# Attention logits of heads 1 to 7 by way of a DRAM row, an earlier load of two vectors, and two sums moved, in a two-layer graph attention kernel

## The chip, the core and the metric

The kernel runs on one core of one Trainium2 chip. The metric is the device time of one launch in microseconds (us). A core has TensorE (PE, with its weight loads shown apart as PEld), VectorE (DVE), ScalarE (ACT), GpSimd (POOL) and SyncE (SP, which here only issues DMAs), and 16 DMA engines that all queues share. Each engine runs its own instructions in order and waits for others on semaphores.

## The reference

A residual block over 512 nodes with 768 features: `layernorm(x + GAT(x))`, where GAT has two attention layers over the same edges. The first has 8 heads, whose outputs stand side by side (512 x 6144), the second one head.

```python
h = (x @ W).reshape(n, H, C)
alpha_s = jnp.einsum('nhc,hc->nh', h, a_s)          # source logits
alpha_d = jnp.einsum('nhc,hc->nh', h, a_d)          # destination logits
e = jax.nn.leaky_relu(alpha_s[src] + alpha_d[dst], NEG_SLOPE)
m = jax.ops.segment_max(e, dst, num_segments=n)
e = jnp.exp(e - m[dst])
denom = jax.ops.segment_sum(e, dst, num_segments=n)
alpha = e / (denom[dst] + EPS)
out = jax.ops.segment_sum(h[src] * alpha[:, :, None], dst, num_segments=n)
...
h = jax.nn.elu(gat_layer(x, W1, a_src1, a_dst1, b1, edge_index, concat=True))
out = gat_layer(h, W2, a_src2, a_dst2, b2, edge_index, concat=True)
```

## The kernel before

The edges are turned once into a dense 512 x 512 matrix of counts, `cnt`, with a mask `absent` beside it. Each head is then dense work: its projection, a 512 x 512 matrix of attention weights, their product, ELU, and its part of the second layer's product, which is summed over the heads in `h2` and `u2`. Nodes lie in 4 tiles of 128 partitions.

The attention matrix of a head needs the destination logit of a node as one value for each partition (`AL[h][1]`) and the source logits of all 512 nodes along the free axis, the same on every partition (`BC[h]`). The source logits come out of VectorE as a 128 x 4 tile, `AL[h][0]`. `spread(h)` (L360) makes `BC[h]` from it on TensorE: four transposes of a column that is broadcast to 128 x 128, into one PSUM bank. Then for each tile of nodes `lift` (L366, ACT: destination minus source logits), `leak` (L372, DVE), `rank` (L375, DVE and an exponential on ACT) and `weigh` (L525, DVE, with `cnt` as factor). `turn_out` and `turn_in` transpose the result by DMA into `PT`.

Large products are done by Strassen's scheme in the form with seven products: `left`, `right`, `left_sums` and `right_sums` return the operands and a list of VectorE sums that some of them need. `second` and `projection` return 14 pairs each, of a product and of the VectorE or ScalarE step that empties its bank. P2 is added to the bank of P1, so P2 waits until the step that empties P1 has read it; P4 and P3 stand likewise on P7 and P5.

The order of the work is written out by hand: the program's order is each engine's order, and there is no scheduler. The loop over `h` (L678), here called pass 0 to pass 6, does this:

1. SP issues the weights `load_w1(h + 2)`: `w2t` (the piece t1) and six rows of blocks, each 384 KB, into buffers that the products of the projection before must have left. POOL issues two more DMAs that add onto what has landed (L104, L115).
2. `mixed` (L603): attention product of head `h` and ELU. Between its steps VectorE takes entries of the list `fill`: the sums that are still open and the logits of head `h + 1` (`half_logits`, L256). After it `load_a` loads the logit vectors of head `h + 2`. The last pass, 6, uses `aggregate` instead of `mixed`; VectorE then does the logits of head 7 and twelve products of the second layer's vectors with rows of its weights (L703), which fill `V`.
3. `second(h)`: its pairs P1 are issued (`m()`), then on VectorE the step that empties the first bank (`pairs[0][1]`), the last ELU steps (`finish`), the sums `gsums[0]` and `gsums[1]`, and the step for the second bank (`pairs[1][1]`, L306, or L304 where the bank starts a sum). TensorE does `spread(h + 1)` after its P1 products, then the two products of P2, P6, P7, P4, P5, P3. The attention matrix of head `h + 1` is made beside them.
4. The projection of head `h + 2`.

In pass 0 the start differs: the last products of head 1's projection (L667 on) run beside the end of head 0's attention matrix, and the lists `beside` set what VectorE and ScalarE do at each of them. `rsums` are four sums over `PT` that the second product of `mixed(0)`, P6, needs the first two of. `some_logits` are two half logits of head 1.

In pass 6 SP issues `load_w2(7)` (t1 and six blocks), then the two vectors `a_src2` and `a_dst2` of the second layer (L686). All SP loads stand in one queue; DMA issues of SP rotate through eight semaphores, so that a DMA is not issued before the one eight places ahead of it has landed.

Of the kernel before, what the change touches and what calls it, by code (L numbers as in the profile page):

```python
# [8 lines left out]
F32 = mybir.dt.float32  # L9
# [3 lines left out]
U16 = mybir.dt.uint16  # L13
# [23 lines left out]
def gat_pass(  # L37
# [16 lines left out]
    nc = tc.nc  # L54
    P = 128
    N, D = x.shape
    H = a_src1.shape[0]
    E = src.shape[0]
    NT = N // P
# [11 lines left out]
    keep = ctx.enter_context(tc.tile_pool(name="keep", bufs=1))  # L71
    wpool = ctx.enter_context(tc.tile_pool(name="weights", bufs=1))
    hpool = ctx.enter_context(tc.tile_pool(name="hpool", bufs=2))
    small = ctx.enter_context(tc.tile_pool(name="small", bufs=4))
    qpool = ctx.enter_context(tc.tile_pool(name="qpool", bufs=4))
    counting = ExitStack()
    ohp = counting.enter_context(tc.tile_pool(name="onehot", bufs=1))
    mm = ctx.enter_context(tc.tile_pool(name="mm", bufs=5, space=bass.MemoryType.PSUM))
    tr = ctx.enter_context(tc.tile_pool(name="tr", bufs=2, space=bass.MemoryType.PSUM))
    bc = ctx.enter_context(tc.tile_pool(name="bc", bufs=1, space=bass.MemoryType.PSUM))  # L80
    def row_bcast(ap_row):
        return bass.AP(tensor=ap_row.tensor, offset=ap_row.offset, ap=[[0, P], [1, D]])

# [12 lines left out]
    def load_w(W, h, slot, m):  # L98


        t1 = wpool.tile([P, HK, HALF], F32, name=f"{slot}t1")
        upper = m[:HK * P, :].rearrange("(k p) d -> p k d", p=P)
        nc.sync.dma_start(t1, upper[:, :, L])
        nc.gpsimd.dma_start(t1, upper[:, :, R], accum_op=ALU.add)  # L104
        W[h] = []
        for r in range(2):
            w = wpool.tile([P, HK, D], F32, name=f"{slot}{r}")
            for k in range(r * HK, (r + 1) * HK):
                nc.sync.dma_start(w[:, k - r * HK, :], m[k * P:(k + 1) * P, :])
            W[h].append(w)  # L110
        W[h].append(t1)

        def rest():

            nc.gpsimd.dma_start(W[h][0][:, :, R], m[HK * P:, R].rearrange("(k p) d -> p k d", p=P),  # L115
                                accum_op=ALU.add)
        return rest
# [4 lines left out]
    def load_w2(h, slot="w1"):  # L122
        return load_w(W2, h, slot, w2[h * D:(h + 1) * D, :])
# [81 lines left out]
        nc.vector.scalar_tensor_tensor(below, rel, float(W), below, op0=ALU.is_ge, op1=ALU.add,  # L205
                                       accum_out=stray)

    cnt = keep.tile([P, NT, N], F32, name="cnt")
    absent = keep.tile([P, NT, N], BF16, name="absent")
    xT = keep.tile([P, DC, N], F32, name="xT")  # L210
    xS = keep.tile([P, 3, HK, HN], F32, name="xS")
# [11 lines left out]
    def left(aT, s):  # L223
        a11, a12 = aT[:, :HK, :HN], aT[:, HK:, :HN]
        a21, a22 = aT[:, :HK, HN:], aT[:, HK:, HN:]
        tt = nc.vector.tensor_tensor
        return dict(P1=a11, P2=a12, P3=s[:, 2], P4=a22, P5=s[:, 0], P6=s[:, 1], P7=a21), [
            lambda: tt(s[:, 0], a21, a22, op=ALU.subtract),
            lambda: tt(s[:, 1], s[:, 0], a11, op=ALU.subtract),
            lambda: tt(a21, a11, a21, op=ALU.subtract),  # L230
            lambda: tt(s[:, 2], a12, s[:, 1], op=ALU.add),
        ]
# [18 lines left out]
    HS, AL, BC = {}, {}, {}  # L251
# [108 lines left out]
    def spread(h):  # L360
        BC[h] = bc.tile([P, 512], F32, name="bc")
        for t in range(NT):
            nc.tensor.transpose(BC[h][:, t * P:(t + 1) * P],  # L363
                                AL[h][0][:, t:t + 1].to_broadcast([P, P]), ident)

    def lift(h, t):  # L366

# [30 lines left out]
    if not general:  # L398
# [5 lines left out]
        cps, done = {}, 0  # L404
# [111 lines left out]
    late = ctx.enter_context(tc.tile_pool(name="late", bufs=1))  # L516
# [35 lines left out]
    def turn_in(t):  # L552
        nc.scalar.copy(PT.rearrange("p s n -> p (s n)").bitcast(U16).rearrange("p (s n h) -> p s n h", s=NT, h=2)[  # L553
            :, :, t * P:(t + 1) * P, :], parted.pop(t).rearrange("p (h s d) -> p s d h", h=2, s=NT))
# [99 lines left out]
    AA, lsums = left_sums(0)  # L654
    BB, rsums = right_sums()
    some_logits = half_logits(1, 2)

    def give(t):
# [3 lines left out]
    done = {n: (lambda n=n: pairs[n][1]()) for n in range(4, 13)}  # L662
    beside = {4: [lambda: give(0)], 5: [done[4]], 6: [done[5]], 7: [done[6], lambda: give(1)],
              8: [done[7], lambda: leak(q[3]), lambda: rank(q[3], 3), lambda: turn_in(0)], 9: [lambda: give(2), done[8]],
              10: [lambda: give(3), lambda: turn_in(1), done[9]], 11: [done[10], lsums[0]],
              12: [done[11], lambda: turn_in(2), *lsums[1:3]], 13: [done[12], some_logits[0], lambda: turn_in(3)]}
    for n in range(4, 14):  # L667
        pairs[n][0]()
        for f in beside[n]:
# [2 lines left out]
            load_w2(0)()  # L672
            B2, pending = right(W2[0], "w1")
    pairs[13][1]()
    for f in rsums:
        f()
    besides = [lsums[3], some_logits[1]]
    for h in range(H - 1):  # L678
        if h + 2 < H:
            load_w1(h + 2)()  # L680
        else:
            last_sum = load_w2(H - 1, "w2")
            A[H] = []
            for j, a in ((2, a_src2[0]), (4, a_dst2[0])):
                v = wpool.tile([P, HK, HALF], F32, name=f"w2t{j}").rearrange("p k n -> p (k n)")[:, :D]
                nc.sync.dma_start(v, row_bcast(a))  # L686
                A[H].append(v)
        GA, gsums = left(gT, gS)
        if h + 2 < H:
            finish = mixed(h, AA, BB, besides + [p for t in ((0, 1) if h else (0, 1, 3)) for p in half_logits(h + 1, t)])  # L690
        else:
            finish = []
            for c in range(DC):
                finish.append(aggregate(h, c))
                if c:
                    finish.pop(0)()
                if c < 2:
                    logits(h + 1, HS[h + 1], c)
                else:

                    for k in ((0, 1), (2,), (3,), (4, 5))[c - 2]:
                        for v, a, sign in zip(range(2), A[H], (1.0, -1.0)):
                            nc.vector.scalar_tensor_tensor(scr, W2[H - 1][k // HK][:, k % HK, :], sign, a,  # L703
                                                           op0=ALU.mult, op1=ALU.mult, accum_out=V[:, k, v:v + 1])
        besides = []
        if h + 2 < H:
            load_a(h + 2, a_src1[h + 2], a_dst1[h + 2])
        pairs = second(h, GA, B2)
        for m, _ in pairs[:2]:
            m()  # L710
        pairs[0][1]()
        for f in finish:
            f()
        gsums[0]()
        gsums[1]()
        pairs[1][1]()
        if pending:
            pending.pop(0)()
        spread(h + 1)
        pairs[2][0]()  # L720
        gsums[2]()
        pairs[3][0]()
        gsums[3]()
        if pending:
            pending.pop(0)()
        pairs[2][1]()
        pairs[3][1]()
        last = h + 2 == H
        q = [lift(h + 1, 0)]
        for n in range(2, 7):  # L730
            (m0, e0), (m1, e1) = pairs[2 * n:2 * n + 2]
            m0()
            if not last:
                m1()
            if n < 6:
                leak(q[n - 2])
                rank(q[n - 2], n - 2)
            if n < 5:
                q.append(lift(h + 1, n - 1))
            if last:  # L740

                if n > 3:
                    turn(q[n - 4], n - 4)
                if n == 6:
                    weigh(q[3], 3)
                m1(lambda: turn(q[3], 3) if n == 6 else None)
            if not last and n == 6:
                turn_in(0)
                weigh(q[2], 2)
                turn_out(q[2], 2)  # L750
            e0()
            if last and 2 < n < 6:
                weigh(q[n - 3], n - 3)
            if not last and 3 < n < 6:
                weigh(q[n - 4], n - 4)
                turn_out(q[n - 4], n - 4)
            if not last and n == 6:
                weigh(q[3], 3)
                turn_out(q[3], 3)
                load_w2(h + 1)()  # L760
            e1()
        if h + 2 < H:
            B_, sums = right(W1[h + 2], "w2")
            pairs = projection(h + 2, XA, B_)
            for n in range(14):
                pairs[n][0]()
                if n == 0:
                    turn_in(1)
                    B2, sums2 = right(W2[h + 1], "w1")
                if n in (1, 3):  # L770
                    sums[n // 2]()
                if n == 1:
                    AA, sums3 = left_sums(h + 1) if h + 3 < H else (None, [])
                pairs[n][1]()
                if n in (2, 4):
                    turn_in(1 + n // 2)
                if n == 5 and h + 3 < H:
                    BB, sums3 = right_sums()
                if 1 <= n < 9 and h + 3 < H:
                    sums3.pop(0)()  # L780
                if n in (9, 10):
                    sums2.pop(0)()
                if n in (11, 13):
                    logits(h + 2, HS[h + 2], 2 + (n - 11) // 2)
        else:
            last_sum()
            B2, sums2 = right(W2[H - 1], "w1")
# [151 lines left out]
```

## Time and profile before

| | |
|---|---|
| time, median of 3 runs (lowest, highest) | 661.86 us (660.59, 662.08) |
| the profiled execution's own time | 662.61 us |
| its span from first to last instruction | 660.8 us |
| PE busy, share of the span | 649.1 us, 98% |
| DVE busy | 511.7 us, 77% |
| ACT busy | 248.6 us, 38% |
| mean granted TensorE clock | 0.996 |
| a transpose of `spread`, PE MATMUL L363 | 274 ns mean, 32 of them, 4.8 us in all |
| an SP load of a logit vector (a_s, 384 KB), median to landing | 3.5 us |

The profiled execution is 0.75 us above the median of the runs, and 1.8 us of its time lie outside the span. A row of the timeline gives the start, the duration, the engine, the line and the operation, the tiles written and read, the number of instructions merged, and in brackets the engine's idle time before it with what ended it. Matmul records overlap: a 128 x 384 matmul has a record of 0.49 us but follows the one before after 0.32 us, and a transpose of 128 x 128 after 0.11 us.

### The profile page before, as it was taken

To read this page: it belongs to the slowest core of one execution; us is meant where nothing else is said; L and a number is where in the kernel's file an instruction comes from. 1 tells how busy PE (TensorE), PEld (TensorE's weight loads), DVE (VectorE), ACT (ScalarE), POOL (GpSimd) and SP (SyncE) were. 2 spreads that over 40 slices of the span, in tenths; PEclk is the share of its full clock that TensorE was granted. 3 is DMA by queue.
4 is the path that set the end of the run, shared out by engine and by line. 5 is a ranking of instruction groups with operands and counts; after the bars stand their busy time and mean duration, and the time that the engine had idled before them with its cause. 6 is when DMAs were issued, how large, how long until landed. Compare 5 with 4: busy or idle time off the path is not lost.

```text
span 660.8 us, 7107 instructions
## 1 busy us (share of the span) xinstructions
PE 649.1 (98%) x2419; PEld 401.1 (61%) x2419; DVE 511.7 (77%) x1102; ACT 248.6 (38%) x417; POOL 42.8 (6%) x52
## 2 busy tenths in 40 slices
PE   8999999999999999999999999999999999999995
PEld 4555567556865577556855586557755544644553
DVE  6979989977779587767688687868785579866785
ACT  2222646350635135440725035430735042333440
POOL 1300011010100110010000110011000000000000
PEclk9999999999999999999999999999999999999998
DMA  8801299177803882087605790196506674000122
GB/s 308 239 1 49 33 277 285 28 220 160 225 1 68 246 236 64 16 248 189 160 0 129 185 273 26 33 264 202 116 0 194 158 225 132 24 0 1 28 61 76
DMA packets 71355, 85.58 MB, mean 130 GB/s; under 512 B 36566, under 2 KB 55950, under 8 KB 71310
## 3 DMA queue, kind: packets, MB, share of 16 engines
q1 hardware_dynamic: 59022, 66.76, 32.2%
q0 software_dynamic: 12000, 17.70, 15.8%
q10 hardware_dynamic: 288, 0.59, 0.3%
q8 instruction: 21, 0.34, 0.2%
q14 instruction: 24, 0.20, 0.1%
HBM read 75.07 MB, written 1.57 MB: 116 GB/s over the span
## 4 chain that ended last, share of the span: by engine, by line
PE 93%; DMA 3%; DVE 2%; issue 1%; SPq 0%; ACT 0%; DVEq 0%
PE mm L248 61%; PE mm L625 17%; PE mm L352 5%; PE mm L571 3%; PE mm L891 3%; PE tr L430 2%; DMA w2t<-in_L_gnn_a_dst_dram 2%; DMA hs<-in_x_dram 1%; DVE scr L703 1%; PE bc L430 1%; PE bc L363 0%; DVE gT L565 0%; PE mm L327 0%; PE tr L819 0%; PE tr L540 0%
## 5 line engine op out<-in xcount | busy, mean ns | idle before, releaser
L248 PE MATMUL mm<-w,gT 128*128 128x384 f32 x288 | 97.8, 488 | 1.4 <-DVE u L306 1.4
L248 PE MATMUL mm<-w,xT 128*128 128x384 f32 x252 | 83.9, 487 | 0.0
L248 PEld LDWEIGHTS mm<-w,gT 128*128 128x128 f32 x288 | 53.4, 190 | 38.2 <-DVE u L306 3.9
L248 PEld LDWEIGHTS mm<-w,xT 128*128 128x128 f32 x252 | 47.7, 190 | 33.7 <-issue 0.4
L248 PE MATMUL mm<-w1t,gS 128*128 128x384 f32 x180 | 60.7, 486 | 0.0
L380 ACT ACTIVATE q<-q,nmax 128x512 f32<-128x512 f32 x36 | 25.8, 721 | 91.6 <-DVE nmax L378 91.6
L248 PE MATMUL mm<-w2t,xS 128*128 128x384 f32 x168 | 56.6, 487 | 0.0
L625 PE MATMUL mm<-PT,hs 128*128 128x256 f32 x216 | 52.5, 379 | 0.0
L629 ACT COPY u<-mm 128x256 f32<-128x256 f32 x18 | 6.7, 372 | 119.1 <-PE mm L625 119.1
L306 DVE TENSOR_TENSOR h<-h,mm 128x384 f32<-128x384 f32 x72 | 39.7, 551 | 13.9 <-PE mm L248 12.7
L248 PEld LDWEIGHTS mm<-w1t,gS 128*128 128x128 f32 x180 | 34.1, 190 | 23.6
L248 PEld LDWEIGHTS mm<-w2t,xS 128*128 128x128 f32 x168 | 31.8, 190 | 22.2 <-issue 0.2
L625 PEld LDWEIGHTS mm<-PT,hs 128*128 128x128 f32 x216 | 41.0, 190 | 6.9
L548 ACT COPY nr<-q 128x1024 uint16<-128x1024 uint16 x32 | 33.4, 1044 | 22.4 <-DVE q L534 15.5
L571 PE MATMUL mm<-PT,hs 128*128 128x512 f32 x96 | 41.6, 593 | 0.0
L418 DVE TENSOR_SCALAR os<-nodes,idx 128x512 bf16<-128x512 f16 x132 | 35.8, 343 | 4.1 <-PE tr L430 4.0
L625 PE MATMUL mm<-pS,gS 128*128 128x256 f32 x144 | 37.1, 380 | 1.1 <-DVE pS L598 1.1
L553 ACT COPY PT<-zr 128x1024 uint16<-128x1024 uint16 x32 | 37.1, 1159 | 2.0 <-DMA zr<-nr 2.0
L352 PE MATMUL mm<-w,xT 128*128 128x384 f32 x96 | 33.3, 493 | 0.0
L248 PE MATMUL mm<-w,gS 128*128 128x384 f32 x96 | 32.6, 486 | 0.0
L248 PE MATMUL mm<-w1t,gT 128*128 128x384 f32 x96 | 32.5, 487 | 0.0
L571 PEld LDWEIGHTS mm<-PT,hs 128*128 128x128 f32 x96 | 18.2, 190 | 22.9 <-issue 21.5
(158 smaller groups left out, 1030.2 us busy)
## 6 DMA issues: line engine op xcount, KB each, us to landing
w<-in_L_gnn_W_dram SPq DMA_DIRECT2D x90, 384.0 KB, 6.1
w<-in_L_gnn_W_dram POOLq DMA_DIRECT2D x15, 576.0 KB, 8.9
w2t<-in_L_gnn_W_dram SPq DMA_DIRECT2D x8, 576.0 KB, 4.7
w2t<-in_L_gnn_W_dram POOLq DMA_DIRECT2D x8, 576.0 KB, 8.8
w1t<-in_L_gnn_W_dram SPq DMA_DIRECT2D x7, 576.0 KB, 4.5
w1t<-in_L_gnn_W_dram POOLq DMA_DIRECT2D x7, 576.0 KB, 9.4
a_s<-in_L_gnn_a_src_dram SPq DMA_DIRECT2D x8, 384.0 KB, 3.5
a_d<-in_L_gnn_a_dst_dram SPq DMA_DIRECT2D x8, 384.0 KB, 3.4
```

The source lines that it names most:

```text
L248: nc.tensor.matmul(ps[:, :HALF], A_[p][:, k, i * P:(i + 1) * P], B_[p][:, k, :], start=start and k == 0, stop=k == HK - 1, skip_group_chec ...
L306: nc.vector.tensor_tensor(a, a, ps, op=ALU.subtract if p == "P7" else ALU.add)
L352: nc.tensor.matmul(ps, xT[:, r * HK + k, t * P:(t + 1) * P], W1[h][r][:, k, cols], start=r == 0 and k == 0, stop=r == 1 and k == HK - 1)
L380: nc.scalar.activation(q, q, AF.Exp, bias=nmax, scale=-1.0)
L418: nc.vector.tensor_scalar(hot[c], nodes, idx[:, 1, c:c + 1], None, op0=ALU.is_equal)
L430: nc.tensor.matmul(cps[t][r:r + B, :N], od[:, c, k * B:(k + 1) * B], hot[c], start=todo[b] == hits[b], stop=todo[b] == 1, tile_position=(0 ...
L548: nc.scalar.copy(apart.rearrange("p (h n) -> p h n", h=2), q.bitcast(U16).rearrange("p (n h) -> p h n", h=2))
L553: nc.scalar.copy(PT.rearrange("p s n -> p (s n)").bitcast(U16).rearrange("p (s n h) -> p s n h", s=NT, h=2)[:, :, t * P:(t + 1) * P, :], p ...
L571: nc.tensor.matmul(ps[:, :N], HS[h][:, s, c * P:(c + 1) * P], PT[:, s, :], start=(s == 0), stop=(s == NT - 1))
L625: nc.tensor.matmul(bank[p][:, :HN], A_[p][:, k, c * P:(c + 1) * P], B_[p][:, k, :], start=over is None and k == 0, stop=k == 1, skip_group ...
L629: nc.scalar.copy(u, part("P1"))
L891: nc.tensor.matmul(ps[:, :cols.stop - cols.start], PT[:, s, t * P:(t + 1) * P], h2[:, s, cols], start=(s == 2), stop=(s == 1))
```

## The change

For heads 1 to 7 `spread(h + 1)` is gone from TensorE. A new `bounce(h + 1)` stands between `mixed` and `load_a`: SP writes the 128 x 4 source logits into a DRAM row of 512 floats (one element of 4 bytes at a time, since the row is transposed on the way), waits until it has landed, and reads the row back onto all 128 partitions of an SBUF tile. Head 0 keeps `spread`. `cnt` becomes a 16-bit tile, half its size. In pass 6 the two vectors are loaded ahead of the weights. In pass 0 the first two of `rsums` come one step earlier, ahead of the step that empties the projection's last bank, and `some_logits[0]` goes from there into the list of `mixed(0)`, which then has nine entries in place of eight.

```diff
+    dram = ctx.enter_context(tc.tile_pool(name="dram", bufs=2, space=bass.MemoryType.DRAM))
...
-    def row_bcast(ap_row):
-        return bass.AP(tensor=ap_row.tensor, offset=ap_row.offset, ap=[[0, P], [1, D]])
+    def row_bcast(ap_row, n=D):
+        return bass.AP(tensor=ap_row.tensor, offset=ap_row.offset, ap=[[0, P], [1, n]])
...
-    cnt = keep.tile([P, NT, N], F32, name="cnt")
+    cnt = keep.tile([P, NT, N], U16, name="cnt")
...
+    def bounce(h):
+
+        row = dram.tile([NT, P], F32, name="row")
+        nc.sync.dma_start(row.rearrange("t p -> p t"), AL[h][0])
+        BC[h] = late.tile([P, N], F32, name="bc")
+        nc.sync.dma_start(BC[h], row_bcast(row, N))
...
-              12: [done[11], lambda: turn_in(2), *lsums[1:3]], 13: [done[12], some_logits[0], lambda: turn_in(3)]}
+              12: [done[11], lambda: turn_in(2), *lsums[1:3]], 13: [done[12], lambda: turn_in(3), *rsums[:2]]}
...
-    for f in rsums:
+    for f in rsums[2:]:
         f()
-    besides = [lsums[3], some_logits[1]]
+    besides = [lsums[3], *some_logits]
...
         else:
-            last_sum = load_w2(H - 1, "w2")
             A[H] = []
             for j, a in ((2, a_src2[0]), (4, a_dst2[0])):
                 v = wpool.tile([P, HK, HALF], F32, name=f"w2t{j}").rearrange("p k n -> p (k n)")[:, :D]
                 nc.sync.dma_start(v, row_bcast(a))
                 A[H].append(v)
+            last_sum = load_w2(H - 1, "w2")
...
         besides = []
+        bounce(h + 1)
         if h + 2 < H:
             load_a(h + 2, a_src1[h + 2], a_dst1[h + 2])
...
-        spread(h + 1)
         pairs[2][0]()
         gsums[2]()
```

## The prediction

> **What bounds the kernel.** The page's busy times come first, then the chain of waits, then the timeline around each place that the diff touches.
>
> ```profile
> PE 649.1 (98%) x2419; PEld 401.1 (61%) x2419; DVE 511.7 (77%) x1102; ACT 248.6 (38%) x417; POOL 42.8 (6%) x52
> ```
>
> TensorE is busy almost throughout, so an edit pays only where it takes work off TensorE that nothing else then fills with a wait, or removes one of its few waits. The chain of waits gives each `spread` 0.44 us of TensorE (four transposes, a matmul every 0.11 us); seven are removed, so 3.1 us is the naive gain. Whether it is one is told by what the weight loads of L248 wait for, with total, times and longest:
>
> ```profile
> PEld mm L248 <- DVE u L306: 3.9, 7, 1.5
> ```
>
> Seven waits for L306, the step that empties the first banks of `second`. Two are in pass 6 (0.78 and 1.46 us). The other five are 0.34 us each, one in each of passes 1 to 5. This is one of them, pass 1:
>
> ```profile
> 184.22 0.55 DVE L306 TENSOR_TENSOR u<-u,mm 128x384 f32<-128x384 f32 x1 [1.51 <-PE mm L248]
> ...
> 185.96 0.60 PE L363 MATMUL bc<-ident,al_s 128*128 128x128 f32 x4
> ...
> 187.62 0.55 DVE L306 TENSOR_TENSOR u<-u,mm 128x384 f32<-128x384 f32 x1
> ...
> 188.22 1.60 PEld L248 LDWEIGHTS mm<-w,gT 128*128 128x128 f32 x6 [0.34 <-DVE u L306]
> ```
>
> The reader is to see a race. VectorE starts when TensorE ends the first P1 product (184.2) and runs six operations without a gap: L306, two ELU steps, two sums of 0.96, the second L306, which ends at 188.17. TensorE meanwhile does the second P1 product, `spread`, and the first P2 product, then needs that second L306. It arrives exactly on time: the weight load starts 0.05 us after it, and the matmul follows its predecessor at the usual 0.32 us.
>
> **Passes 1 to 5: `spread` goes.** TensorE would be ready 0.44 us earlier, but the second P2 product still starts when L306 has ended, and L306 follows from the first P1 product, which does not move. The wait of 0.34 becomes 0.78. I take 0.01 us for each pass, 0.05 in all, instead of 5 x 0.44 = 2.2. The bounds are 0 and 2.2.
>
> What is added there: SP writes the row when the source logits are ready (the L257 step that ends at 174.7) and reads it back; `lift` needs it so that L373 can start at 190.94. Two issues pass ahead of `load_a`, which moves from 174.7 to about 179; its vectors are read some 50 us later in the projection, and SP's next transposes are issued at 203, so this costs nothing. POOL's accumulating DMA is still moving until 176.8. Even at 0.135 us for each small packet (the 3 KB packets of q1 beside q0), 32 to an engine: 176.8 + 4.3 + 0.5 for landing, then 2.9 for the read, then `lift` with 0.8, is 185.3. The cover is 5.6 us. `cnt` in 16 bits: L378, which reads the 16-bit `absent`, takes 691 ns, L528 with 32-bit `cnt` 684; nothing.
>
> **Pass 6: the vectors first.**
>
> ```profile
> 539.89 0.96 DVE L703 SCALAR_TENSOR_TENSOR scr<-w,w2t 128x768 bf16<-128x768 f32 x1 [1.61 <-DMA w2t<-in_L_gnn_a_src_dram]
> ...
> 541.37 0.96 DVE L703 SCALAR_TENSOR_TENSOR scr<-w,w2t 128x768 bf16<-128x768 f32 x1 [0.52 <-DMA w2t<-in_L_gnn_a_dst_dram]
> ...
> 547.23 0.63 ACT L564 ACTIVATE nr<-nr 128x512 f32<-128x512 f32 x1
> ...
> 557.36 1.59 PEld L248 LDWEIGHTS mm<-w,gT 128*128 128x128 f32 x6 [1.46 <-DVE u L306]
> ```
>
> The vectors are issued at 530.2 and 530.7 behind seven weight DMAs and land at 539.8 and 541.3. Their buffers are free when the products P6 and P4 of head 7's projection are done, the later by 521.1 (528.9 less four products of 1.94), and the DMA share is 0.00 from 522 to 526; at 3.5 us to landing they are there by 525, before the weights are even issued. So both waits of VectorE, 2.1 us, go. Step by step: L703 follows L565 (537.59) by 0.60, so 538.19; four at 1.00; the next L565 at 542.1 instead of 544.3, the next at 544.6 instead of 546.7. The third would start at 547.0, but its ACT step (third line) ends at 547.86: what is late next. It starts at 547.9 instead of 549.2, and 1.31 of the 2.1 remain. The rest follows at the same distances, and the weight load at 557.36 comes at 556.05. TensorE, free of P1 at 553.3 and of the first P2 product at 555.2, still waits 0.85 there, so this `spread` is swallowed as well. Gain **1.31 us**, with 1.0 and 2.1 as bounds. The row for head 7 is issued at 535.8 and needed at 558.8.
>
> **Pass 0: sums sooner, and the bounce under load.**
>
> ```profile
> 91.10 0.73 PEld L625 LDWEIGHTS mm<-pS,gS 128*128 128x128 f32 x4 [1.51 <-DVE pS L598]
> ...
> 111.11 0.56 DVE L304 TENSOR_SCALAR u<-mm 128x384 f32<-128x384 f32 x1 [0.64 <-PE mm L248]
> ...
> 115.11 1.59 PEld L248 LDWEIGHTS mm<-w,gT 128*128 128x128 f32 x6 [0.34 <-DVE u L304]
> ...
> 120.18 0.68 DVE L373 SCALAR_TENSOR_TENSOR q<-q 128x512 f32<-128x512 f32 x1
> ```
>
> L597 needs the last `turn_in` (ACT, ends 88.68), so it starts at 88.73 instead of 89.64; L598 ends at 90.14, and P6 starts at 90.19 instead of 91.10. But L287 now stands before L599, which P7 needs: it ends at 91.22, and P7 starts about 0.72 early (91.35 for 92.07). `mixed(0)` keeps that 0.72. At its end VectorE has one half logit more (0.99 us), of which 0.64 falls into the idle time before L304; L304 starts at 110.80 for 111.11. From there VectorE is full until L373, and the second P2 product waits for it (0.34 now), so TensorE too is **0.31 us** ahead, not 0.72 + 0.44.
>
> Now the row. The last source logit of head 1 is written at 109.75 and the row is issued at 109.85, while the weights of two loads are still moving. L373 wants `lift` by 119.87. The a_s load issued at 107.64 took 8.2 us to land, one at 466.7 took 3.3. Why is seen in the DMA queues between 110 and 111.5 (packets, MB, share of 16 engines):
>
> ```profile
> q0 software_dynamic: 149, 0.23, 87.0%
> q1 hardware_dynamic: 56, 0.13, 26.7%
> ```
>
> q0 is POOL's accumulating DMA, q1 is SP's. SP's loads find q0 at work, and by the packet records a_s and a_d (issued 107.64 and 110.50) begin some 3.5 us after issue; an a_d alone (469.57) begins after 0.93. So the row begins at about 113.3. It is 512 elements of 4 bytes: the Trainium skill ("DMA: Bandwidth & Descriptors", Rules for kernel authors) has one descriptor per element where the last dimension is strided, so 32 on each engine; no row here shows such a transfer. Price of one: 0.02 us from below (the transposes' 256-byte packets run at 19 ns), 0.135 from above; I take 0.02, the nearer in size. Beside q0 they alternate. From 107.5 to 110 q0 moved 174 packets and q1 170, one for one. Two engines lag (their share of the last weight block lands at 113.6), and have about 22 q0 packets of 0.139 left: 22 x 0.16 + 10 x 0.02 = 3.7, so 117.0; 0.6 to landing (the output's last packets land after 0.5), 117.6. The read, 256 KB: 0.1 for the issue, 0.93 to begin, 1.2 (two thirds of a_d's 1.75), 0.7 to land: 120.5. `lift` 0.67 and hand-over: 121.3, **1.4 us late**. L373 stands first of a full queue: L378, the steps for P6, L304 for P7, on which P4's weight load waits already (0.46 at 124.90). So TensorE loses all of it.
>
> The same page (Queues, rings and completion order) has an engine change queues by packets of typically 9 to 17 descriptors. By that rule the row passes in at most four turns, 0.6 us of q0 instead of 3.1: BC is there at about 118, nothing is late, and the sum is 1.67. By the rows it is 0.27. Descriptors of 1.5 and 3 KB went singly here, so I take the rows.
>
> **Sum.** 0.05 + 1.31 + 0.31 - 1.4 = 0.27 us gained: the profiled 662.61 becomes 662.3, and the median, 0.75 below it, **661.6**. About 0.2%, 1.3 us, is what a measurement of this kernel can tell from no change.
>
> **Rivals.**
> - *A, forecast*: the bounce is 0.35 to 3.0 us late in pass 0 and eats the gain of pass 6; 660.5 to 663.2. Chance 0.40.
> - *B, nothing late*: packets of many descriptors, or an earlier begin. 1.67 us, 660.2. For: POOL's queue runs alone until the row begins and may be nearly empty by then. Against: 8.2 us for a single load at that place. 0.22.
> - *C, `spread` pays in passes 1 to 5*: 0.43 x 5 more, 659.4, or 658.0 with B. For: the chain names L363 with 0.5% of the span. Against: the five waits of 0.34. 0.12.
> - *D, slower*: the 4-byte writes are dear. At 0.1 us each, 22 x 0.139 + 32 x 0.1 = 6.3 us: landed at 120.2, read by 123.1, 3.9 late, a loss of 2.3: 664.2. It decides from 1.67 us of lateness (0.03 us for each descriptor gives 1.7), and shows from 3.0. At 0.135 it is 5.1 late, 665.3. For: two DMAs in a row under the heaviest load. 0.26.
>
> Faster is B and C, 0.34; within 0.2% A, 0.40; slower D, 0.26. The range, 659.2 to 664.3, takes in B, D's middle and part of C.
>
> **What will show it.** In passes 1 to 5 the wait for L306 grows from 0.34 to about 0.78 and TensorE's stretch keeps its 73 us from pass to pass. In pass 6 L703 no longer waits for a DMA, and one L565 waits for ACT. In pass 0 P6 starts near 90.2, L304 near 110.8, and L373 waits for `lift`, which waits for the DMA of `bc`. A period shorter than 72.9 us would refute the first step; L373 at 119.9 the last.

## The result

| | before | after |
|---|---|---|
| time, median (lowest, highest) | 661.71 us (660.59, 662.08), 6 runs | 672.17 us (671.12, 672.78), 6 runs |
| ratio, with its 95% interval | | 1.0158 (1.0145 to 1.0171) |
| the profiled execution's own time | 662.61 us | 672.44 us |
| its span; mean granted clock | 660.8 us; 0.996 | 670.7 us; 0.991 |

The change makes the kernel 10.5 us slower. The forecast was 661.6, with a range up to 664.3: the sign is that of rival D, the size over four times the 2.3 us that D gives.

**Where it went.** The span can be cut at work that both kernels do. The table gives each stretch in the profiled executions, from rows of the timeline: pass 0 runs from the first matmul of `mixed(0)` to that of `mixed(1)`, passes 1 to 5 from there to the first matmul of `aggregate` in pass 6, pass 6 from there to the first matmul of layer 2's `aggregate`, and the end from ACT's issue of the last output DMA to the end of the span.

| stretch | before, us | after, us | difference |
|---|---|---|---|
| up to `mixed(0)` | 88.96 | 89.10 | +0.1 |
| pass 0 | 74.75 | 83.43 | **+8.7** |
| passes 1 to 5 (73.0 each in both) | 364.99 | 364.96 | 0.0 |
| pass 6 | 52.00 | 50.66 | **-1.3** |
| layer 2 | 75.18 | 75.19 | 0.0 |
| end | 4.95 | 7.33 | **+2.4** |

Three views of after follow. First the busy times, then lines of the waits (engine, line and tile that waited, for what: us in all, times, longest):

```profile
PE 650.4 (97%) x2391; PEld 399.9 (60%) x2391; DVE 512.3 (76%) x1102; ACT 249.5 (37%) x417; POOL 43.2 (6%) x52
```

```profile
ACT q L377 <- DMA bc<-row: 26.5, 6, 14.7
...
DVE q L381 <- ACT q L377: 8.3, 4, 6.8
PEld mm L249 <- DVE h L305: 7.4, 1, 7.4
...
PE mm L249 <- DVE h L305: 6.8, 1, 6.8
...
PEld mm L249 <- DVE u L307: 5.5, 7, 1.4
...
PE mm L249 <- DVE u L307: 1.6, 6, 0.8
```

TensorE has 28 matmuls fewer and is busy 1.3 us longer, which already hints at a slower clock. The waits of 14.7, 6.8 and 6.8 are one chain in pass 0. (In after, lines stand 1 to 8 further down: L305 is L304 of before, L307 is L306, L377 the ACT step of `lift`, L381 `leak`.) The timeline of after shows it:

```profile
110.00 0.39 SPq L370 DMA_DIRECT2D row<-al_s  x1
...
110.89 0.55 DVE L305 TENSOR_SCALAR u<-mm 128x384 f32<-128x384 f32 x1
...
114.89 1.59 PEld L249 LDWEIGHTS mm<-w,gT 128*128 128x128 f32 x6 [1.06 <-DVE u L305]
...
120.76 0.33 SPq L372 DMA_DIRECT2D bc<-row  x1
...
126.08 0.72 ACT L377 ACTIVATE q<-bc,al_d 128x512 f32<-128x512 f32 x1 [14.69 <-DMA bc<-row]
126.84 0.69 DVE L381 SCALAR_TENSOR_TENSOR q<-q 128x512 f32<-128x512 f32 x1 [6.80 <-ACT q L377]
...
131.61 5.61 PE L249 MATMUL mm<-w1t,gT 128*128 128x384 f32 x10 [6.78 <-DVE h L305]
```

Row written at 110.0, read back at 120.8, there at 126.1; VectorE stands in front of L381 for 6.80 us with P7's emptying step (L305) queued behind it; P4, which adds onto P7's bank, starts 6.78 us late. When it starts, the matmuls are slow. The windows of after (columns: stretch; busy us and instructions of PE, PEld, DVE, ACT, POOL; granted clock; DMA share; GB/s):

```profile
120.00:124.00 4.00, 4.00 (x13) 2.30 (x13) 0.04 (x1) 0.00 (x0) 0.00 (x0) 1.00 0.15 15
124.00:128.00 4.00, 0.83 (x3) 0.19 (x1) 1.13 (x2) 0.72 (x1) 0.00 (x0) 1.00 0.76 247
128.00:132.00 4.00, 0.39 (x1) 0.39 (x2) 3.50 (x9) 2.21 (x4) 0.00 (x0) 0.64 0.00 0
132.00:136.00 4.00, 4.00 (x7) 2.13 (x7) 1.55 (x5) 1.79 (x3) 0.00 (x0) 0.51 0.00 0
136.00:140.00 4.00, 4.00 (x14) 2.32 (x13) 3.82 (x11) 1.21 (x2) 0.00 (x0) 1.00 0.00 0
```

The reader is to see seven matmuls in 132 to 136 where a stretch at full clock has 14, both with PE "busy" for 4.00 us: the clock fell to about half after the pause. Before, the same stretch shows:

```profile
132.00:136.00 4.00, 4.00 (x14) 2.31 (x13) 3.79 (x13) 2.88 (x3) 0.00 (x0) 1.00 0.37 72
```

Why the row took 10.7 us is told by the DMA traffic of after in the window from 110 to 121 us (its first row is the busy share of the 16 engines in 40 slices of 0.275 us, in tenths; the last is the row's DMA with the time from issue to landing):

```profile
DMA  9999999999999999999421000000000000000000
...
row<-al_s SPq DMA_DIRECT2D x1, 2.0 KB, 10.7
```

After slice 22 next to nothing moves. By the packet records the row's packets, mostly of 9 or 24 ns, begin at 113.7, 3.7 us after the issue, and the last goes at 116.5, **sooner** than forecast (117.0). But the DMA lands at 120.75, 4.2 us later. The same view of pass 1, from 183.5 to 192, where nothing else is loaded but the last of POOL's DMA:

```profile
DMA  9999999551000000000000000000000000000000
...
row<-al_s SPq DMA_DIRECT2D x1, 2.0 KB, 8.5
```

Packets stop after slice 10 (the last at 185.7), and it lands 6.3 us later, at 192.0. So most of the time here is neither in the queue nor in the packets but behind them.

Passes 1 to 5 of after, here pass 1 at the same place as shown of before:

```profile
195.56 0.96 DVE L230 TENSOR_TENSOR gS<-gS,gT 128x768 f32<-128x768 f32 x1
196.44 0.55 DVE L307 TENSOR_TENSOR u<-u,mm 128x384 f32<-128x384 f32 x1
...
197.04 1.59 PEld L249 LDWEIGHTS mm<-w,gT 128*128 128x128 f32 x6 [0.78 <-DVE u L307]
197.04 2.20 PE L249 MATMUL mm<-w,gT 128*128 128x384 f32 x6 [0.16 <-DVE u L307]
```

The wait is 0.78, as forecast, and now the matmul waits too, which it did not before: the 0.44 us of `spread` has become idle time of TensorE. (The bracket shows 0.16, since the record before it overlaps; from start to start the two matmuls here take 0.65 and 0.43 us in place of 0.32 each.)

Pass 6 of after:

```profile
546.37 0.69 DVE L573 SCALAR_TENSOR_TENSOR gT<-nr,zr 128x512 f32<-128x512 f32 x1 [0.80 <-ACT nr L572]
546.98 0.95 DVE L711 SCALAR_TENSOR_TENSOR scr<-w,w2t 128x768 bf16<-128x768 f32 x1
```

L711 (L703 of before) starts 0.61 after L573 and no longer waits for a DMA.

### The profile page after: what moved, and what is told of

It is laid out like the page before. It is cut to its first block, busy times and chain, and to the rows that moved or that the text cites. A ratio compares the mean times of both kernels' runs of the same rounds, so it can differ in the third digit from the quotient of the medians.

```text
span 670.7 us, 7073 instructions
## 1 busy us (share of the span) xinstructions
PE 650.4 (97%) x2391; PEld 399.9 (60%) x2391; DVE 512.3 (76%) x1102; ACT 249.5 (37%) x417; POOL 43.2 (6%) x52
## 4 chain that ended last, share of the span: by engine, by line
PE 87%; DVE 7%; DMA 3%; ACT 1%; issue 1%; DVEq 0%; ACTq 0%
PE mm L249 52%; PE mm L633 16%; PE mm L579 6%; PE mm L353 5%; PE mm L899 3%; PE tr L438 2%; DMA row<-al_s 2%; DVE u L307 1%; PE bc L155 1%; DVE gS L229 1%; DVE gS L230 1%; DVE gT L573 1%; DMA bc<-row 1%; PE bc L438 1%; DVE q L381 1%
## 5 line engine op out<-in xcount | busy, mean ns | idle before, releaser
L307 DVE TENSOR_TENSOR h<-h,mm 128x384 f32<-128x384 f32 x72 | 39.7, 551 | 13.8 <-PE mm L249 12.6
L633 PEld LDWEIGHTS mm<-PT,hs 128*128 128x128 f32 x216 | 41.0, 190 | 7.2 <-issue 0.4
L249 PE MATMUL mm<-w1t,gT 128*128 128x384 f32 x96 | 34.7, 512 | 6.8 <-DVE h L305 6.8
L377 ACT ACTIVATE q<-bc,al_d 128x512 f32<-128x512 f32 x32 | 22.3, 707 | 30.0 <-DMA bc<-row 26.5
```

The source lines that it names most:

```text
L249: nc.tensor.matmul(ps[:, :HALF], A_[p][:, k, i * P:(i + 1) * P], B_[p][:, k, :], start=start and k == 0, stop=k == HK - 1, skip_group_chec ...
L307: nc.vector.tensor_tensor(a, a, ps, op=ALU.subtract if p == "P7" else ALU.add)
L377: nc.scalar.activation(q, BC[h][:, :N], AF.Identity, bias=AL[h][1][:, t:t + 1], scale=-1.0)
L633: nc.tensor.matmul(bank[p][:, :HN], A_[p][:, k, c * P:(c + 1) * P], B_[p][:, k, :], start=over is None and k == 0, stop=k == 1, skip_group ...
```

## Experiments

Times are medians; each is compared with runs of the kernel before on the same chip (661.5 to 661.7). "Pass 0", "pass 6" and "end" are the stretches of the table above.

| kernel | time, us | ratio to before (95%) | pass 0 | each of passes 1 to 5 | pass 6 | end |
|---|---|---|---|---|---|---|
| before | 661.71 | | 74.75 | 73.00 | 52.00 | 4.9 |
| after | 672.17 | 1.0158 (1.0145 to 1.0171) | 83.43 | 72.99 | 50.66 | 7.3 |
| e1 head 1 by TensorE | 662.78 | 1.0016 (1.0010 to 1.0023) | 74.36 | 72.99 | 50.67 | 6.7 |
| e2 vectors first alone | 661.17 | 0.9992 (0.9984 to 1.0001) | 74.74 | 73.00 | 50.67 | 5.2 |
| e3 sums sooner alone | 661.35 | 0.9996 (0.9989 to 1.0003) | 74.38 | 73.00 | 50.98 | 5.0 |
| e4 row for heads 2 to 7 alone | 662.93 | 1.0025 (1.0012 to 1.0038) | 74.75 | 72.99 | 50.67 | 6.5 |
| e5 row in pieces of 16 bytes | 663.62 | 1.0027 (1.0016 to 1.0039) | 75.00 | 72.99 | 50.67 | 7.1 |
| e13 row in pieces of 8 bytes | 666.32 | 1.0082 (1.0057 to 1.0106) | 76.57 | 72.99 | 50.66 | 7.2 |
| e6 wait filled | 670.11 | 1.0126 (1.0111 to 1.0142) | 81.44 | 72.99 | 50.67 | 7.2 |
| e9 longer SP program | 670.26 | 1.0130 (1.0115 to 1.0146) | 84.45 | 72.99 | 50.67 | 5.0 |
| e7 VectorE's order alone | 661.40 | 0.9999 (0.9991 to 1.0008) | 75.16 | 73.00 | 50.26 | 5.1 |
| e10 order, vectors, sums | 660.59 | 0.9983 (0.9977 to 0.9990) | 74.39 | 73.00 | 50.08 | 5.3 |
| e11 e1 and order | 659.45 | 0.9972 (0.9962 to 0.9981) | 74.36 | 72.56 | 49.64 | 7.0 |
| e12 e11 and longer SP program | **657.75** | 0.9940 (0.9927 to 0.9954) | 74.38 | 72.56 | 49.64 | 5.2 |

### Each part by itself

Head 1 back on TensorE, the rest of the change kept:

```diff
-        bounce(h + 1)
+        if h:
+            bounce(h + 1)
...
+        if h == 0:
+            spread(h + 1)
         pairs[2][0]()
```

> The changed kernel with one part undone: head 1's logits are spread by TensorE as before, heads 2 to 7 by way of the DRAM row. Theory L (the whole loss starts with the one bounce of pass 0, which lands 7 us late under the weight loads; the slower clock of 132 to 136 follows from the wait): pass 1 begins at 163.5 to 163.9, granted clock 1.00 there, the gain of pass 6 stays, and the time is 660.3 to 661.2 if the end of the run is as before, up to 2.4 more if the late end (4.5 us from the last landing to the end of the span) comes with any bounce. Rival M (bounces cost something in every pass, or the 16-bit counts do): still slower than before, 664 or more, with passes longer than 73.0.

662.78. Pass 0 is 74.36, 9.07 less than in after and 0.39 less than in before: the loss of pass 0, wait and clock, is that one bounce. The late end stays, so it belongs to something else that the change brings.

The vectors first, alone (the diff of the change, these lines only):

```diff
-            last_sum = load_w2(H - 1, "w2")
             A[H] = []
...
                 A[H].append(v)
+            last_sum = load_w2(H - 1, "w2")
```

> The kernel before with one part of the change alone: the layer-2 vectors are loaded ahead of head 7's layer-2 weights in pass 6. Theory L: the two waits of L703 for DMA go, the step from pass 6 to the end shortens by 1.3 us: 660.3 to 660.6 on 661.7. Rival: the vectors' issue waits for their buffers and holds the weight loads back behind it on SP, so that the last sums of layer 2 are late and nothing is gained: 661.5 or more.

661.17: a gain of 0.4 by the medians, and by the interval between a loss of 0.1 and a gain of 1.1. The expected 1.3 is not there, although the profile of this kernel shows pass 6 at 50.67 against 52.00. The reason is in e3 and e4, which still load the vectors behind the weights: their pass 6 takes 50.98 and 50.67. This is L703 of e3, in its timeline:

```profile
537.89 0.95 DVE L703 SCALAR_TENSOR_TENSOR scr<-w,w2t 128x768 bf16<-128x768 f32 x1
...
540.04 0.96 DVE L703 SCALAR_TENSOR_TENSOR scr<-w,w2t 128x768 bf16<-128x768 f32 x1 [1.19 <-DMA w2t<-in_L_gnn_a_dst_dram]
```

One wait of 1.19 where the profile of before has 1.61 and 0.52; e4 has one of 0.27. When the vectors land behind seven weight DMAs differs from one profiled execution to the next, and that of before was a late one.

The two sums sooner, alone:

```diff
-... 13: [done[12], some_logits[0], lambda: turn_in(3)]}
+... 13: [done[12], lambda: turn_in(3), *rsums[:2]]}
...
-    for f in rsums:
+    for f in rsums[2:]:
...
-    besides = [lsums[3], some_logits[1]]
+    besides = [lsums[3], *some_logits]
```

> The kernel before with one part alone: two of head 0's sums ahead of the half logit. Theory L: P6 of mixed(0) starts near 90.2, VectorE has one half logit more at the end, and 0.3 us is gained in pass 0: 661.4. Rival (from the changed kernel, where the last source logit of head 1 was ready at about the same time as before and pass 0's VectorE queue stayed full): nothing at all, 661.6 to 661.8.

661.35, which the interval does not tell from before. Pass 0 is 0.37 shorter in this profile and 0.36 to 0.39 in those of e1, e10, e11 and e12, so the gain is there, of the size expected, and too small to be told by the times of the whole kernel.

The row for heads 2 to 7, alone: `bounce` and the 16-bit `cnt` put into the kernel before, called as in e1.

> The kernel before with one part alone: heads 2 to 7 by way of the DRAM row (and the counts in 16 bits), head 1 by TensorE. Theory L: taking four transposes out of passes 1 to 6 moves nothing, because the second P2 product waits for L306 of VectorE: period 73.0, wait for L306 in each of passes 1 to 5 0.78 instead of 0.34, 661.7 plus what the end of the run costs (0 to 2.4). Rival C (spread pays 0.44 each): 659.1 to 659.5. Rival M (bounces cost in every pass): a period above 73.0, 663 or more.

662.93, period 72.99, weight loads waiting 0.78 for L307 in each of passes 1 to 5: removing six `spread`s pays nothing there (rival C of the prediction falls), and the row's landing, 6.6 to 8.9 us after its issue in these passes, is hidden. What is lost is the end, 1.6 us more than in before.

### What makes the row late

The row in 128 pieces of 16 bytes, `lift` reading it in the permuted order:

```diff
-        row = dram.tile([NT, P], F32, name="row")
-        nc.sync.dma_start(row.rearrange("t p -> p t"), AL[h][0])
+        row = dram.tile([P, NT], F32, name="row")
+        nc.sync.dma_start(row, AL[h][0])
...
+            src = src.rearrange("p (n t) -> p t n", t=NT)
```

> The changed kernel with the row written as 128 pieces of 16 bytes (the four logits of a partition side by side) instead of 512 of 4 bytes; the lift reads the bounced tile in the permuted order, so all values are the same. Theory W (what makes the row land late is the number of small writes to DRAM that have to be completed): in passes 1 to 5 the row lands in about 3.5 us instead of 7.9 to 8.6, in pass 0 about 5 to 6 us sooner than 120.7, so the lift is 1 to 2 us late instead of 7.0, and the time is 665 to 667. Rival F (any write to DRAM takes that long to be completed, whatever its pieces): the row still takes 8 us, pass 0 still loses 7, time 672.

663.62. The DMA issues of after and then of e5 (the last number is the median us to landing, over all seven heads):

```profile
bc<-row SPq DMA_DIRECT2D x7, 256.0 KB, 4.9
...
row<-al_s SPq DMA_DIRECT2D x7, 2.0 KB, 8.6
```

```profile
bc<-row SPq DMA_DIRECT2D x7, 256.0 KB, 3.5
...
row<-al_s SPq DMA_DIRECT2D x7, 2.0 KB, 2.9
```

The same 2 KB to DRAM land in a third of the time when they are a quarter as many pieces, each four times as large; pass 0 goes from 83.43 to 75.00. Rival F falls, and the gain is larger than theory W said; that it is the number of pieces and not their size is not shown by this run. By the packet records it is the landing that changes: it follows the last packet after 0.5 to 1.2 us, 0.5 in pass 0, where after has 4.2 to 6.4. In pass 0 the first packet still comes 3.6 us after the issue, yet VectorE does not wait for the first `lift`. What pass 0 still loses against e1, 0.64 us, stands beside a cost of this version itself: read in the permuted order, that `lift` takes 1.24 us instead of 0.72, and the second `leak` waits 1.02 for its own `lift`.

In between, 256 pieces of 8 bytes:

```diff
+        row = dram.tile([2, P, 2], F32, name="row")
+        nc.sync.dma_start(row.rearrange("a p b -> p a b"), AL[h][0].rearrange("p (a b) -> p a b", b=2))
```

> The changed kernel with the row written as 256 pieces of 8 bytes. In passes 1 to 6 the row of 512 pieces landed after 8.2 us (middle of six), that of 128 pieces of 16 bytes after 2.75. Theory W, linear in the number of pieces (14 ns each): 4.6 us in passes 1 to 6, 7.0 in pass 0, lift some 3 us late, 665 to 668. Rival W8 (it is the size of a piece: below 16 bytes a write is dear, whatever their number): the row lands after 8 us as with 4 bytes, or after half of it only if 8 bytes are already cheap (3 us).

666.32. The row lands after 3.85 us in passes 1 to 6 (middle of six; 4.6 expected) and 6.7 in pass 0. From 128 to 256 pieces the landing grows by 1.1 us, from 256 to 512 by 4.35. So it is not linear in the number. Number and size were not varied apart, and how much each of them does stays open.

### The slow clock

The wait filled with products that nothing uses:

```diff
+            if h == 0 and n == 4:
+                idle = bc.tile([P, 512], F32, name="bc")
+                for _ in range(10):
+                    nc.tensor.matmul(idle[:, :HALF], ident, xT[:, 0, :HALF], start=True, stop=True)
             m0()
```

> The changed kernel with ten products of the identity by the input's transpose (6.45 us of TensorE) put before P4 of pass 0, into the PSUM bank that spread no longer uses; their result is used by nothing. Theory K (the slower clock of 0.51 to 0.64 between 128 and 136 comes from TensorE standing still for 6.8 us): the wait stays as long, but is filled; P4 runs at 0.32 us a matmul from its first, and pass 1 begins 2.0 to 2.3 us sooner than 172.5: about 670.0. Rival: the clock falls for another reason (the whole chip is throttled there): still 0.5 to 0.65 around 132 to 136, and 672.

670.11, and the windows of e6 in the place of the slow ones:

```profile
128.00:132.00 4.00, 3.54 (x12) 1.85 (x11) 3.50 (x9) 2.14 (x4) 0.00 (x0) 1.00 0.00 0
132.00:136.00 4.00, 4.00 (x14) 2.30 (x13) 3.40 (x11) 1.86 (x3) 0.00 (x0) 1.00 0.00 0
```

The clock stays at 1.00 and pass 0 is 1.99 us shorter. So of the 9.07 us that the bounce costs pass 0, 7.1 are the wait and 2.0 the clock that falls because of it. In e13, where TensorE waits 2.0 us at the same place, the windows from 124 to 136 all show 1.00. The loss is not a fixed one: in e9, which has the same bounce and a wait of 6.9 us, the four windows from 124 to 140 show 0.85, 0.50, 0.50 and 0.87, and pass 0 is 1.0 us longer than in after.

### The late end

A longer program for SP, with the same work:

```diff
-            nc.sync.dma_start(t_[:, t, :], x[t * P:(t + 1) * P, :])
+            for half in (L, R):
+                nc.sync.dma_start(t_[:, t, half], x[t * P:(t + 1) * P, half])
```

> The changed kernel with the four loads of x ahead of layer 2 issued as eight halves, so that SP's program is four issues longer (and four more in the copy that is branched over). Theory I (the 2.1 us more between the last landing and the end of the span is an instruction fetch: SP's code crosses a block just behind its jump to the end, and the block boundary moves with the number of SP's instructions): the end of the run goes back from 4.5 to about 2.4 us after the last landing, 670.0. Rival D (it is the price of having written to DRAM, a completion that the end waits for): still 4.5, 672.

670.26. Before, after and e9, the issue of the last output DMA (the spans are 660.8, 670.7 and 668.5):

```profile
655.88 0.36 ACTq L908 DMA_DIRECT2D out_dram<-hs  x1
```

```profile
663.34 0.36 ACTq L916 DMA_DIRECT2D out_dram<-hs  x1
```

```profile
663.56 0.36 ACTq L917 DMA_DIRECT2D out_dram<-hs  x1
```

From after to e9: same work, issue 0.2 later, end 2.1 earlier, and e9 writes the DRAM rows as after does. The trace shows what ends last: SP's semaphore records at the end of after run 666.25, 666.35, then nothing until 668.56; in e1 the gap comes after the sixth of them, in e4 after the eighth, and before has none. With 319, 317 and 316 SP records in after, e1 and e4, the gap stands at one fixed place of SP's program: each record fewer puts it two later (each SP issue is in the program twice, since the whole kernel is repeated behind a branch). The other traces agree: e5, e6 and e13 (319) have the gap after the second record, e11 (317) after the sixth, and e9 (324) and e12 (322) have none. Theory I holds as far as the position goes. That the gap is a fetch of code is not shown: an 8 KB packet of the instruction queue starts inside each of these three gaps, but such packets move at the end of before too, where SP has no gap. The Trainium skill ("Runtime: NRT & Kernel Launch", Instruction fetch mechanics) says that a taken branch out of the window held by an engine forces a fetch before it can go on. SP does branch to the end here, though the gap lies a few instructions behind the branch's target.

### VectorE's order, and a version that beats both

```diff
+        pairs[1][1]()
         gsums[0]()
         gsums[1]()
-        pairs[1][1]()
```

> The kernel before with one line moved: VectorE's second L306 of second (it empties the second P1 bank) stands ahead of the two sums of 0.96 us that stood before it. Theory V (the second P2 product waits for VectorE's order, which is why taking spread away paid nothing): the wait of 0.34 goes in passes 1 to 5 (1.7 us in all), the like in pass 6 (0.8 to 1.5), period 72.65: 658.3 to 659.3. Rival: VectorE is full there, the sums come too late for P6 and the wait moves to it: 661.5.

661.40: theory V, as worded there, falls. The wait of the weight load for L306 is gone in passes 1 to 5 and the period is 73.00 as before. The mistake was mine: in before the *matmuls* of this place follow one another at 0.32 us, so the 0.34 is time in which the next weights could have been loaded early, not time that TensorE lost. In pass 0 the matmuls of P4 now wait 0.4 for L304 and the pass is 0.41 longer; in pass 6 some is gained.

Then the order in passes 1 to 6 only, with the two other cheap parts, and `spread` for all heads:

> The kernel before with the vectors first, head 0's sums sooner, and VectorE's second L306 ahead of the two sums in passes 1 to 6; every head is spread by TensorE. Theory V: TensorE has no matmul gap in passes 1 to 5 anyway (0.32 us from matmul to matmul), so the new order pays nothing there and the period stays 73.0; 0.35 from pass 0 and 0.4 to 0.8 from pass 6: 660.3 to 660.8. Rival (the parts don't add, since the end of pass 6 waits for something else): 661.2 or more.

660.59, as expected. And the same order with TensorE free of `spread` for heads 2 to 7 (e1 with that line moved):

> The changed kernel with head 1 spread by TensorE (as in the first experiment, 662.8) and in passes 1 to 6 VectorE's second L306 ahead of the two sums. Theory V (the 0.44 us of a spread is TensorE's own time, and came back as a wait for L306 only because of VectorE's order): now the wait goes too, the period is 72.56 in passes 1 to 5, pass 6 gains as well: 2.2 to 2.8 less than the first experiment, 660.0 to 660.6, with the late end of the run still in it. Rival (another engine or the weight loads keep the period at 73.0): 662.4 to 662.8.

659.45, 3.3 less than e1, more than expected: the period falls to 72.56 and pass 6 to 49.64. The timeline of e11 in pass 1:

```profile
182.64 6.61 PE L249 MATMUL mm<-w,gT 128*128 128x384 f32 x20
...
185.42 0.56 DVE L307 TENSOR_TENSOR u<-u,mm 128x384 f32<-128x384 f32 x1 [0.44 <-PE mm L249]
...
185.90 0.95 DVE L229 TENSOR_TENSOR gS<-gT 128x768 f32<-128x768 f32 x1
```

The second L307 now waits for TensorE, not TensorE for it, and 20 matmuls run without a break. Either half alone (e4, e7) is worth nothing in passes 1 to 5; together they give 0.44 us a pass.

> The same with the loads of x ahead of layer 2 issued as eight halves, so that SP's program is longer [...]. Theory I: the end of the run is 2.3 us after SP's first wait there instead of 4.0: 1.7 less than the run without it, 658.3 to 658.9, faster than both kernels. Rival (the fetch only moves to another place on the path): no less than 660.

657.75, a little better than expected, ratio to before 0.9940 (0.9927 to 0.9954): 4.0 us faster than before and 14.4 faster than after.

## Why the prediction was wrong

**The step that failed: the price of the row in pass 0**, "the row begins at about 113.3 ... so 117.0; 0.6 to landing (the output's last packets land after 0.5), 117.6". Begin and packets were good: the row's packets start at 113.7 and end at 116.5, the price of 0.02 us for a small one holds, and beside POOL's queue they go one for one (from 114.0 to 114.8 q0 and q1 move 103 packets each), so that the packets of many descriptors in rival B do not show. The 0.6 was 4.2. It came from a row of the trace that is not near: the output goes to DRAM in pieces of 1.5 KB, the row in pieces of 4 bytes. For pieces of 16 bytes it would have been right (0.5 in pass 0 of e5). And the bounds put the whole uncertainty into the time of a packet (0.02 to 0.135 us), while the packets were quick and the landing slow. Of rival D's price, "the 4-byte writes are dear", the direction was right and the place wrong. The read-back was mis-sized too: 5.3 us from issue to the start of `lift`, 2.9 in the sum; its packets begin 2.7 us after the issue, where 0.93 was taken, and no run shows why (0.96 in e5). The row landed 3.1 us later than forecast and the read took 2.4 longer, so the lateness was 7.0 us instead of 1.4 (126.84 against 119.87 for L381).

The Trainium skill would have warned: "DMA: Bandwidth & Descriptors" (Anatomy of one DMA) has a fixed cost of about 2 us for a DMA (given there for POOL's path; this row is SP's), most of it the confirmation of the last write, and says that this "can cause a surprisingly long delay especially when the write target is HBM". An estimate with 2 us in place of 0.6 would have put the row at 119.0 and the lateness near 3 us; the runs say 4.2 after the last packet, so the page's figure is too small for 512 pieces of 4 bytes, and not far off for 128 of 16 as the whole way from issue to landing (e5: 2.3 to 3.4 in passes 1 to 6).

**The clock.** That a wait of some us on TensorE is followed by matmuls at half speed was missing from every rival. The range of lateness in D reached 5.1 us, so it belonged there. The skill has the rule ("TensorE: Matmul & The Clock Gate", HAM oscillation): no idle gap of TensorE beyond about 3.4 us. The runs agree: 2.0 us idle cost no clock, 6.8 us gave 0.64 and 0.51 in the windows from 128 to 136; where between the two the step lies was not measured. By rule and row D should have had a step of some 2 us more once the wait passes 3.4.

**The end.** 2.4 us that no view of before shows, and that had no term in the sum. In these runs it goes with how many instructions SP's program has, not with what they do.

**Passes 1 to 5: right**, in mechanism and size: wait 0.78, period 72.99, and rival C refuted by e4 and e11 together, since `spread` does cost 0.44 of TensorE but VectorE's order takes it back. The room was smaller than counted: in pass 1 of after the row and its read took 13.3 us from the first issue where 9.8 was allowed, so of the cover of 5.6 us some 2.1 was left.

**Pass 6: the mechanism right, the credit wrong.** L711 waits for no DMA, one L573 waits for ACT (0.80), and against the profile of before the stretch is 1.34 shorter (1.31 forecast). But that profile was one late execution; e3 and e4 have 50.98 and 50.67 with the vectors still behind the weights. The step "the median, 0.75 below it" then took much of the same lateness off twice: pass 6 of the execution shown was 1.0 to 1.3 longer than in these two, with the very wait whose removal was counted in full.

**Pass 0, sums sooner: right.** P6's weights load at 90.33 with `mixed` 0.14 later than in before (90.2 forecast), L305 at 110.89 (110.80), and 0.37 gained in e3 (0.31). What was costed at nothing was nothing: `load_a`, held back behind the row in every pass, keeps no one waiting, and `weigh` takes 685 ns with the 16-bit `cnt`, 684 before.

As sums: +8.7 for pass 0, -1.3 for pass 6, +2.4 for the end, +0.1 ahead of it, is 9.8, the difference of the two profiled times.

## To carry over

A round trip through DRAM is priced from issue to landing, with a row that writes pieces of the same size to the same memory; here the packets were gone 4 to 6 us before the landing. Work taken off the busiest engine pays only if its next wait moves too: look at the gap between matmuls, not at the wait of a weight load, and try the two edits together. Before a wait seen in one profile is counted as gain, ask whether it is the same in a second execution.

## Not expected

- A row of 512 floats in 4-byte pieces lands 7.2 to 8.7 us after its issue in passes 1 to 6 and 10.7 under the weight loads, in 8-byte pieces 2.9 to 4.3 and 6.7, in 16-byte pieces 2.3 to 3.4 and 5.2.
- Where TensorE waited 6.8 us the granted clock was 0.64 and 0.51 in the stretches 128 to 132 and 132 to 136; where it waited 2.0 us it stayed 1.00.
- Some twenty instruction records more on SP (319 for 298), an engine with nothing to compute, went with an end of the kernel about 2 us longer; five more still took that away.
